# The output projection of six blocks: seven half-size products in float32 replaced by three full-size passes in float32r

## The chip, the core and the metric

The kernel runs on one NeuronCore of a Trainium2 chip. The core has a matrix engine (TensorE, "PE" in the profile; its weight loads are listed apart as "PEld"), a vector engine (VectorE, "DVE"), a scalar engine (ScalarE, "ACT"), a general engine (GpSimd, "POOL") and a queue from which most transfers are issued (SyncE, "SP"). Every engine takes its instructions in the order of the program; engines wait for each other through semaphores. SBUF is the on-chip memory, PSUM the banks that PE writes its sums to, DRAM the memory off the core. The metric is the device time of one execution, in microseconds (us).

## The reference

The input x has 4 sequences of 1024 rows of 512 float32 numbers. The part that matters here, with D = 512 and rows as tokens:

```python
h   = layernorm(x)
q, v, g = h @ Wq.T, h @ Wv.T, silu(h @ Wg.T)
ret = scan over the tokens of a sequence: state = lam * state + v
y   = (layernorm(q * ret) * gamma + lnb) * g
o   = y @ Wo.T                                  # the output projection
x1  = x + layernorm(o)
out = x1 + layernorm(ffn(layernorm(x1)))        # gate and up 512 -> 1536, down 1536 -> 512
```

The weights of the feed-forward part are rounded to 8-bit floats first; all else is float32, and the results have to agree with float32.

## The kernel before

**Blocks and turns.** The 4096 rows are 8 blocks of 512. The main loop (`for t in range(NB)`) makes 8 turns of 12 steps `i`. Turn t does the feed-forward part `f` of block t. Between its matmuls stands the attention part `b` (class `Retention`) of block t+1, the end `l` of the feed-forward part of block t-1 (scaling, normalising, adding, storing), and the preparation `n` of block t+2 (loading x, normalising, turning). The order of all instructions on each engine is the order in which this loop writes them. A step is: the matmuls `gate(i)` (8), a gap for a piece of `b`, `up(i)` (8), DVE's `fuse(i)` with a cast on ACT and later the remainder `rest(i)` on DVE, the "mid" gap, `down(i-2)` (8), and in some steps an "end" gap. `gate` and `up` take turns in two PSUM banks; ACT's silu frees the one, DVE's fuse the other.

**The attention part of blocks 2 to 7** (`fast`) uses two ways for v, q and g. Blocks 2 and 3 use a Winograd scheme in plain float32: seven products of half-size matrices per projection, taken from the list `order`, each 8 matmuls over 128x256, with DVE adds (`mids`) between them that read a PSUM bank before the next product adds to it. Blocks 4 to 7 (`by_parts`) use three float32r passes: each operand is cut by a mask into an upper part of 12 bits and a low rest. Pass "top" multiplies the upper parts, "low" the low parts (scaled), ACT scales the bank by 1 + 2^-12, and "diff" adds the product of two differences. A float32r matmul is one instruction over 128x512. For x the parts are made by `low_of` (mask and subtraction on DVE) and `diff_of` (DVE); for the weights by the class `Splitter` in turns 1 to 3, which stores them in DRAM.

**The output of blocks 2 to 7** is made in turns 1 to 6 by the Winograd scheme (`("o", j)`, function `product`): `y_sums` makes four sums of pieces of y (two on DVE, two on POOL), seven products stand in the gaps of steps 7 to 9, and `add_o` moves each bank into the SBUF tile `mids` (two copies on ACT, five adds on DVE). `o_moments`, `x1_of` then take mean and variance, normalise on ACT and add to x on POOL. The weights' sums are made once, in step 0 of turn 1 (`output_sums`: four DVE subtractions), and stored in DRAM.

**The ring.** The streamed weights of v, q, g and o come through a ring of four slots in SBUF (`fetch_weights`, `next_unit`). A load is issued on SP when the use of an earlier unit is written; SP issues in order, so it also stands behind whatever SP waits for.

**What stands ahead of the output.** In steps 3 to 6 of each turn: mean of y (`halves` splits the sum into two float32r halves on ACT and DVE, `mean` multiplies them on PE), `center_y` (DVE, squares on ACT, sums on POOL), `halves` again in step 4 for the variance, `var`, a root on ACT and a reciprocal on DVE (`rstd_y`), `scale_y` in step 5, `gate_y` in step 6 (two chunks of y before `up(6)`, two after `fuse(6)`). The last piece of g is finished at the start of step 6. In steps 6 to 8 block t+2's x is normalised (ACT), turned (`send_x`: a DVE transpose, then a transfer to DRAM), fetched turned (`fetch_x`) and, for blocks 4 to 7, masked (`low_of`). In turn 1 ACT also runs 24 searches for overflow in the rounded weights (`find_over`, tiles `seen`).

**x1nT**, the feed-forward part's input (an upper part and a rest), has two buffers of the tag "x1n"; block t's is read by `gate` and `up` of turn t, block t+1's is written from step 11 of turn t.

Of the kernel before, what the change touches and what calls it, by code (L numbers as in the profile page):

```python
# [23 lines left out]
def retention_ffn_sandwich(  # L24
# [134 lines left out]
    def scratch(n):  # L159
        t = big.tile([P, 4, PW], F32, tag="x1n", name=f"scr_{n}", bufs=2)  # L160
        return [t[:, j, :] for j in range(4)]
# [175 lines left out]
    def turn_by_blocks(dst, src, tag, name):  # L337
# [24 lines left out]
    order += [("o", j) for j in (1, 2, 6, 5, 3, 7, 4)]  # L362
    banks = {
        "v": {1: 0, 6: 1, 5: 0}, "q": {1: 1, 6: 0, 5: 1},
        "g": {1: 0, 6: 0, 5: 1}, "o": {1: 0, 6: 1, 5: 0},
# [6 lines left out]
    stream = order * (PARTS - FAST)  # L372
    late_stream = [(k, c, part) for k in "vqg" for c in range(NC) for part in ("top", "low", "diff")]
    late_stream += [("o", j) for k, j in order if k == "o"]
    stream += late_stream * (NB - PARTS)
# [21 lines left out]
    def output_sums():  # L397

        v = woT.rearrange("(c p) f -> p c f", p=P)
        operands["o"] = {1: v[:, 0:2, 0:H], 2: v[:, 2:4, 0:H], 3: v[:, 2:4, H:D]}  # L400
        b11, b12, b21, b22 = (wo_sb[:, i : i + 2, o : o + H] for i in (0, 2) for o in (0, H))
        made["o"] = {5: b11, 7: b12, 6: b22, 4: b21}
        dve.tensor_tensor(b11, b12, b11, ALU.subtract)
        dve.tensor_tensor(b12, b22, b12, ALU.subtract)
        dve.tensor_tensor(b22, b22, b11, ALU.subtract)
        dve.tensor_tensor(b21, b21, b22, ALU.subtract)

    def copy_output_weights():

        operands["late o"] = dict(operands["o"])  # L410
        for j in (1, 2, 3):
            t = dram.tile([P, 2, H], F32, tag=f"sum_o{j}", name=f"dcopy_o{j}", bufs=1)
            sp.dma_start(t, operands["o"][j])
            operands["late o"][j] = t
# [65 lines left out]
    fetched, taken = [0], [0]  # L480
    rings = {}

    def fetch_weights():

        n = fetched[0]
        change = len(order) * (PARTS - FAST)
        if n == len(stream) or (n >= change and taken[0] < change):
            return
        if n == change:
            rings[True] = wpool.tile([P, RING, D], F32R, tag="wv_sb", name="w_ring_parts")  # L490
        ring = rings[n >= change].bitcast(F32)[:, n % RING]
        what = stream[n]
        if len(what) == 2:
            k, j = what
            unit = operands["late o" if k == "o" and n >= change else k][j]
            sp.dma_start(ring.rearrange("p (c f) -> p c f", c=2), unit)
        else:
            sp.dma_start(ring, operands[what[:2]][what[2]])
        fetched[0] += 1

    def next_unit(*what):
        n = taken[0]
        assert stream[n] == what, (stream[n], what)
        taken[0] += 1
        return rings[n >= len(order) * (PARTS - FAST)][:, n % RING]
# [10 lines left out]

    class Retention:


        def __init__(self, t, xt=None):  # L520
# [8 lines left out]
            self.made = 21 if self.by_parts else 0  # L529
            self.bank, self.top = {}, {}  # L530
# [120 lines left out]
        def end(self, k, c):  # L651
# [25 lines left out]
            else:  # L677
                act.activation(mids[:, c], bank, AF.Silu)
# [11 lines left out]
        def mid(self, c):  # L690
            return mids[:, c].rearrange("p h f -> p (h f)")

        def input_sums(self, *which, engine=pool):
# [4 lines left out]
            ts_ = [t_sums[:, k].rearrange("p c (g j) -> p c g j", j=Q) for k in range(4)]  # L698
# [10 lines left out]
        def product(self):  # L709
# [11 lines left out]
            for o in range(2):  # L721
                out_ = bank[:, o]
                if k != "o" and len(self.right[j].shape) == 4:
                    out_ = out_.rearrange("p (g j) -> p g j", j=Q)
                for c in range(2):
                    if k == "o":
                        left, right = self.left[j][:, c, ts(o, P)], w[:, c, :]
                    else:
                        left, right = w[:, c, ts(o, P)], self.right[j][:, c]
                    pe.matmul(  # L730
                        out_, left, right,
                        start=(j in (1, 6, 5) and o == 0 and c == 0), stop=True,
                        skip_group_check=True,
                    )
            fetch_weights()
            if k == "o":
                return self.add_o(j, bank)
# [24 lines left out]
        def y_sums(self, *which):  # L762
            y = self.y
            a11, a12, a21, a22 = (y[:, c : c + 2, ts(h, H)] for h in range(2) for c in (0, 2))
            if self.by_parts and 1 in which:
                self.t_sums = wpool.tile([P, 4, 2, H], F32, tag="wq_sb", name=f"t_sums_{self.t}")
            s1, s2, s3, s4 = ((self.t_sums if self.by_parts else t_sums)[:, k] for k in range(4))
            self.left = {1: a11, 2: a12, 3: s4, 4: a22, 5: s1, 6: s2, 7: s3}
            ops = {
                1: (dve, s1, a21, a22, ALU.add), 2: (dve, s2, s1, a11, ALU.subtract),  # L770
                3: (pool, s3, a11, a21, ALU.subtract), 4: (pool, s4, a12, s2, ALU.subtract),
            }
            for k in which:
                engine, dst, x, y, op = ops[k]
                engine.tensor_tensor(dst, x, y, op)

        def add_o(self, j, bank):

            by_tile = mids.rearrange("p (r s) h f -> p r s h f", r=2)
            c11, c12, c21, c22 = (by_tile[:, r, :, h, :] for r in range(2) for h in range(2))  # L780
            if j == 1:
                act.copy(c21, bank)
            elif j == 2:
                act.copy(c11, bank)
            elif j == 6:
                dve.tensor_tensor(c12, bank, c21, ALU.add)
            elif j == 5:
                dve.tensor_tensor(c22, bank, c21, ALU.add)
            elif j == 3:
                dve.tensor_tensor(c12, bank, c12, ALU.add)  # L790
            elif j == 7:
                dve.tensor_tensor(c22, bank, c22, ALU.add)
            else:
                dve.tensor_tensor(c21, bank, c21, ALU.add)
            if j in (3, 4):
                for s in (0, 1) if j == 3 else (2, 3):
                    self.po[s] = mids[:, s].rearrange("p h f -> p (h f)")

        def take(self, k, o, h, src):
# [28 lines left out]
            else:  # L828
                act.activation(mids[:, 2 * o + h], src, AF.Silu)
# [101 lines left out]
        def gate_y(self, c):  # L931
# [3 lines left out]
            elif self.fast:  # L935
                y = y.rearrange("p (h f) -> p h f", h=2)
                g = mids[:, 2 * (c // 2) : 2 * (c // 2) + 2, c % 2, :]
# [36 lines left out]
        def new_x1nT(self):  # L974


            self.x1nT = big.tile(
                [P, 2, NC, TB], F32R, tag="x1n", name=f"x1nT_{self.t}", bufs=2
            )
            self.pt = {}  # L980
# [302 lines left out]
    for t in range(NB):  # L1283
        f, n = Ffn(a), None
        fast = b is not None and b.fast
        for i in range(NI):
# [45 lines left out]
            if fast and 7 <= i < 10:  # L1332
                b.product()
            if (1, 0) < (t, i) < (3, NI):
                splitter.at(t, i, "start")
            if n and n.by_parts and i == 7:
# [3 lines left out]
                n.send_x(2)  # L1340
            if n and n.by_parts and i == 8:
                n.low_of(0)
                n.low_of(1)
            if t == PARTS - 2 and i == 9:
                for _ in range(RING - 1):
                    fetch_weights()
# [332 lines left out]
```

## Time and profile before

| | |
|---|---|
| median of 3 runs (range) | 946.67 us (945.62 to 948.26) |
| the profiled execution, its span | 943.62 us, 941.8 us |
| PE busy | 915.1 us (97%), 4022 matmuls |
| DVE, ACT, POOL busy | 677.2 (72%), 439.9 (47%), 273.3 us (29%) |
| chain that ended last | PE 58%, DVE 21%, DMA 7%, ACT 5% |
| moved to and from DRAM | 148.14 MB, mean 157 GB/s |

The profile is of one execution; its timeline gives each instruction's start from the span's beginning, its length, its engine, and what it writes and reads (`out<-in`); in brackets, how long the engine stood idle before and who released it. "x8" merges neighbours. A group in the list of costliest work gives busy time, mean length in ns, and idle time before. An engine's share of the span is an average over stages; who waits for whom in a stage is read from its timeline.

### The profile page before, as it was taken

How to read it: one execution, taken by the hardware profiler on the slowest of the kernel's cores; microseconds unless marked ns; L12 is line 12 of the kernel's file. 1: busy time of each engine (PE TensorE's matmuls, PEld its weight loads, DVE VectorE, ACT ScalarE, POOL GpSimd, SP SyncE). 2: the span in 40 equal slices, each digit the busy share in tenths (PEclk: the TensorE clock that was granted, in tenths of full speed). 3: DMA queues.
4: the chain of work that ended last, by engine and by line, in shares of the span. 5: the costliest groups of instructions: out<-in, count | busy, mean ns of one | idle time of the engine just before them, and what ended most of it. 6: DMA issues, size and time to landing. Idle time of an engine off the chain costs nothing.

```text
span 941.8 us, 11982 instructions
## 1 busy us (share of the span) xinstructions
PE 915.1 (97%) x4022; PEld 754.1 (80%) x4022; DVE 677.2 (72%) x1058; ACT 439.9 (47%) x709; POOL 273.3 (29%) x340
## 2 busy tenths in 40 slices
PE   9999999989999999999999999999999999999996
PEld 7455776678888888888788888888888888888886
DVE  5996999768787886876767856767458765647445
ACT  3556675458666216442263524535264432625323
POOL 1315131321526225240342504323052412314020
PEclk9999999999999999999999999999999999999999
DMA  9302421775638864548856465556555574514021
GB/s 308 129 23 89 134 68 67 193 243 151 189 118 224 257 212 158 199 125 261 275 193 166 125 210 157 168 153 191 174 176 169 132 224 145 157 56 129 6 90 45
DMA packets 115757, 148.14 MB, mean 157 GB/s; under 512 B 10352, under 2 KB 61040, under 8 KB 115696
## 3 DMA queue, kind: packets, MB, share of 16 engines
q1 hardware_dynamic: 114832, 146.72, 50.5%
q8 instruction: 32, 0.52, 0.2%
q10 hardware_dynamic: 864, 0.66, 0.2%
q14 instruction: 29, 0.24, 0.1%
HBM read 108.81 MB, written 42.47 MB: 161 GB/s over the span
## 4 chain that ended last, share of the span: by engine, by line
PE 58%; DVE 21%; DMA 7%; ACT 5%; POOL 3%; SPq 3%; issue 2%; DVEq 0%; ACTq 0%; POOLq 0%
PE pfu L74 11%; PE pfg L74 11%; PE pd L74 9%; PE pq L74 7%; PE pv L74 7%; PE po L74 6%; PE pg L74 5%; DVE y L74 4%; DVE scr L74 3%; SPq L74 3%; DVE st L74 3%; DMA w_ring_parts<-dlow_v 2%; DMA xnT<-mx 2%; DMA mxs<-xs 1%; POOL mv L74 1%
## 5 line engine op out<-in xcount | busy, mean ns | idle before, releaser
L74 PE MATMUL pfu<-x1nT,up_sb 128*128 128x512 f32 x768 | 189.9, 390 | 2.5 <-DVE gate L74 2.5
L74 PE MATMUL pfg<-x1nT,gate_sb 128*128 128x512 f32 x768 | 186.0, 385 | 0.6 <-DVE x1nT L74 0.5
L74 PE MATMUL pd<-down_sb,fuse 128*128 128x512 f32 x720 | 175.4, 386 | 0.0
L74 PEld LDWEIGHTS pfu<-x1nT,up_sb 128*128 128x128 f32 x768 | 144.9, 189 | 27.2 <-DVE gate L74 5.4
L74 PEld LDWEIGHTS pfg<-x1nT,gate_sb 128*128 128x128 f32 x768 | 145.1, 189 | 21.7 <-DVE x1nT L74 1.3
L74 PEld LDWEIGHTS pd<-down_sb,fuse 128*128 128x128 f32 x720 | 141.5, 197 | 14.3
L74 ACT CAST fuse<-gate 128x512 fp32r<-128x512 f32 x90 | 55.5, 616 | 160.0 <-DVE gate L74 159.9
L74 ACT ACTIVATE gate<-pfg,gs_sb 128x512 f32<-128x512 f32 x96 | 65.5, 682 | 94.7 <-PE pfg L74 94.4
L74 DVE SCALAR_TENSOR_TENSOR gate<-pfu,us_sb,gate 128x512 f32<-128x512 f32 x96 | 71.5, 745 | 42.6 <-PE pfu L74 38.9
L74 POOL TENSOR_SCALAR mv<-mv 128x1 f32<-128x1 f32 (+1 forms) x82 | 24.5, 299 | 247.1 <-DVE mv L74 243.6
L74 DVE TENSOR_TENSOR fuse<-gate,fuse 128x512 fp32r<-128x512 f32 x90 | 75.5, 839 | 5.5 <-ACT fuse L74 5.5
L74 DVE BATCH_NORM_STATS2 st<-x 128x6 f32<-128x512 f32 x64 | 43.7, 683 | 22.4 <-POOL x L74 19.8
L74 POOL TENSOR_TENSOR mv<-mv,nhalf 128x1 f32<-128x1 f32 (+1 forms) x75 | 53.3, 710 | 6.3
L74 POOL TENSOR_TENSOR ysum<-y 128x512 f32<-128x512 f32 (+1 forms) x10 | 12.0, 1196 | 144.3 <-DVE y L74 144.2
L74 DVE TENSOR_TENSOR mids<-po,mids 128x512 f32<-128x512 f32 x30 | 20.5, 683 | 38.2 <-PE po L74 38.2
L74 POOL TENSOR_TENSOR x<-x,x1n 128x512 f32<-128x512 f32 x32 | 41.8, 1309 | 15.0 <-ACT x1n L74 14.9
L74 POOL TENSOR_TENSOR d<-d,x 128x512 f32<-128x512 f32 x28 | 35.7, 1296 | 16.5 <-ACT d L74 14.6
L74 POOL TENSOR_TENSOR sqsum<-sqsum,sq 128x512 f32<-128x512 f32 x24 | 34.8, 1448 | 14.6 <-ACT sq L74 12.8
L74 POOL TENSOR_TENSOR ysum<-ysum,y 128x512 f32<-128x512 f32 (+1 forms) x20 | 22.1, 1103 | 47.1 <-DVE y L74 46.7
L74 DVE RECIPROCAL rstd<-rstd 128x512 f32<-128x512 f32 x8 | 26.8, 3352 | 10.7 <-ACT rstd L74 10.7
L74 DVE TENSOR_TENSOR y<-pq,y 128x512 f32<-128x512 f32 x18 | 12.4, 690 | 28.0 <-PE pq L74 28.0
L74 ACT ACTIVATE scr<-scr,neg_low 128x1024 f32<-128x1024 f32 x18 | 20.6, 1144 | 25.5 <-DVE scr L74 25.3
(202 smaller groups left out, 1629.6 us busy)
## 6 DMA issues: line engine op xcount, KB each, us to landing
kept<-x SPq DMA_DIRECT2D x32, 256.0 KB, 2.8
x<-kept SPq DMA_DIRECT2D x32, 256.0 KB, 4.5
x<-in_x SPq DMA_DIRECT2D x28, 256.0 KB, 4.3
out<-d SPq DMA_DIRECT2D x27, 256.0 KB, 2.0
mx<-xs SPq DMA_DIRECT2D x18, 256.0 KB, 2.1
xnT<-mx SPq DMA_DIRECT2D x32, 128.0 KB, 4.7
w_ring_parts<-dtop_v SPq DMA_DIRECT2D x16, 256.0 KB, 3.7
w_ring_parts<-dlow_v SPq DMA_DIRECT2D x16, 256.0 KB, 3.0
```

The lines of the kernel that those rows point to most:

```text
L74: return lambda *args, **kwargs: tc.keep_in_program_order(op(*args, **kwargs))
```

## The change

The output of blocks 2 to 7 is made by three float32r passes, as v, q and g of blocks 4 to 7 are.

- `split_output` (turn 1, steps 0 and 1, two chunks each) makes the three parts of Wo: a mask, a subtraction and a combination on DVE, a copy on ACT, a scaling on POOL. The upper and low parts stay in SBUF, in the first buffer of x1nT; the differences go to DRAM. `output_sums`, the storing of its sums and `copy_output_weights` are gone.
- x1nT of blocks 1 to 7 has one buffer; `new_x1nT` moves from step 8 to step 11.
- `gate_y` of all four chunks stands at the start of step 6. `split_y` (four masks and subtractions on DVE, four copies on ACT) follows `fuse(6)`; `rest_of_y` (four DVE operations) follows `fuse(7)`, ahead of the last `send_x` of step 7.
- `o_gap` puts 48 matmuls into eight gaps of steps 7 to 9. The passes of token tile s go to PSUM bank s mod 2; after pass "low" ACT scales the bank. `o_moments` and `x1_of` read PSUM. They stand in step 8 (start) for tile 0, step 8 (mid) for tile 1; the moments of tile 3 move to the mid of step 9.
- The ring carries four differences per block for o in place of seven units; all four slots are held until the last tile's pass in step 9. When the ring's kind of unit changes (float32 to float32r or back), loading starts once all units of the old kind have been used.
- `mids`, and the sums of x, are taken per block from the tags of wg and wq.
- `halves` for the variance stands before the mid gap of step 4, no longer after it. The end block's `add` of tiles 2 and 3 moves from step 4 to step 5, except in turn 2.

The core of the diff:

```diff
-        t = big.tile([P, 4, PW], F32, tag="x1n", name=f"scr_{n}", bufs=2)
+        t = big.tile([P, 4, PW], F32, tag=f"x1n{n}", name=f"scr_{n}")
...
-    order += [("o", j) for j in (1, 2, 6, 5, 3, 7, 4)]
...
-    late_stream += [("o", j) for k, j in order if k == "o"]
+    last_rests = [("o", c, "diff") for c in range(NC)]
+    by_three = [(k, c, part) for k in "vqg" for c in range(NC) for part in ("top", "low", "diff")]
+    stream = (order + last_rests) * (PARTS - FAST) + (by_three + last_rests) * (NB - PARTS)
...
+    def split_output(c):
+        if c == 0:
+            room = big.tile([P, 2, NC, D], F32R, tag="x1n0", name="wo_parts")
+            wo_parts["top"], wo_parts["low"] = room[:, 0], room[:, 1]
+        w, top, low = wo_sb[:, c], wo_parts["top"][:, c], wo_parts["low"][:, c]
+        cut = work.tile([P, D], F32, tag="tok", name=f"wo_top_{c}", bufs=4)
+        dve.tensor_scalar(cut.bitcast(I32), w.bitcast(I32), TOP_MASK, None, ALU.bitwise_and)
+        dve.tensor_tensor(in_turn(low), as_read(w), as_read(cut), ALU.subtract)
+        act.copy(in_turn(top), as_read(cut))
+        dve.scalar_tensor_tensor(w, top.bitcast(F32), -LOW, low.bitcast(F32), ALU.mult, ALU.add)
+        pool.tensor_scalar(low, low.bitcast(F32), 1.0 / LOW, 1.0, ALU.mult, ALU.mult)
+        t = dram.tile([P, D], F32, tag=f"diff_o{c}", name=f"ddiff_o{c}", bufs=1)
+        sp.dma_start(t, w)
+        operands["o", c] = {"diff": t}
...
+    def fetch_weights(count=1):
+        done[0] += count
+        while fetched[0] < min(done[0] + RING, len(stream)):
+            n = fetched[0]
+            what = stream[n]
+            if n == 0 or len(what) != len(stream[n - 1]):
+                if 0 < n > done[0]:
+                    return
...
+    o_gaps = [
+        [("top", 0), ("top", 1)], [("low", 0), ("low", 1)], [("diff", 0)], [("diff", 1)],
+        [("top", 2), ("low", 2)], [("top", 3), ("low", 3)], [("diff", 2)], [("diff", 3)],
+    ]
...
+        def split_y(self, *chunks):
...
+            for c in chunks:
+                y = self.y[:, c, :]
+                top = work.tile([P, TB], F32, tag="ret", name=f"y_top_{self.t}_{c}")
+                dve.tensor_scalar(top.bitcast(I32), y.bitcast(I32), TOP_MASK, None, ALU.bitwise_and)
+                dve.tensor_tensor(self.y_low[:, c, :], y, top, ALU.subtract)
+                act.copy(self.y_top[:, c, :], top)
+        def rest_of_y(self):
+            self.y_diff = big.tile([P, NC, TB], F32R, tag="y", name=f"y_diff_{self.t}")
+            for c in range(NC):
+                dve.scalar_tensor_tensor(
+                    self.y_diff[:, c, :], self.y_low[:, c, :].bitcast(F32), -1.0 / LOW,
+                    self.y_top[:, c, :].bitcast(F32), ALU.mult, ALU.add,
+                )
...
+        def o_pass(self, part, s):
+            if part == "top":
+                self.po[s] = ps_tile(f"po_{self.t}_{s}", f"pa{s % 2}")
+            left = {"top": self.y_top, "low": self.y_low, "diff": self.y_diff}[part]
+            for c in range(NC):
+                if part != "diff":
+                    w = wo_parts[part][:, c]
+                else:
+                    if s == 0:
+                        self.o_rests[c] = next_unit("o", c, "diff")
+                    w = self.o_rests[c]
+                pe.matmul(
+                    as_read(self.po[s]), left[:, c, ts(s, P)], in_turn(w),
+                    start=part == "top" and c == 0, stop=True, skip_group_check=True,
+                )
+                if part == "diff" and s == NS - 1:
+                    fetch_weights()
+            if part == "low":
+                act.activation(self.po[s], self.po[s], AF.Copy, scale=1.0 + LOW)
...
             if fast and 7 <= i < 10:
-                b.product()
+                b.o_gap(3 * i - 21)
...
+            if fast and i == 8:
+                b.o_moments(0)
+                b.x1_of(0)
             if n and n.by_parts and i == 8:
                 n.low_of(0)
                 n.low_of(1)
...
             if fast and i == 6:
-                b.gate_y(2)
-                b.gate_y(3)
+                for c in range(NC):
+                    b.gate_y(c)
...
-            if fast and i == 7:
-                b.y_sums(3, 4)
...
+            if fast and i == 11:
+                b.new_x1nT()
             f.fuse(i)
...
             if fast and i == 9:
                 b.o_moments(2)
-                b.o_moments(3)
...
+            if fast and i == 4:
+                b.halves()
             if fast and i < 6:
                 b.gap(3 * i + 1, 2 if i == 1 else 1)
...
-            if fast and i == 4:
-                b.halves()
-                l.add(2)
-                l.add(3)
...
+            if fast and i == (4 if t == 2 else 5):
+                l.add(2)
+                l.add(3)
             if fast and i == 6:
-                b.gate_y(0)
-                b.gate_y(1)
-                b.y_sums(1, 2)
+                b.split_y(*range(NC))
+            if fast and i == 7:
+                b.rest_of_y()
...
             if n and n.by_parts and i == 7:
                 n.send_x(3)
-            if fast and i in (7, 8):
-                b.product()
+            if fast and 7 <= i < 10:
+                b.o_gap(3 * i - 20)
+            if fast and i == 9:
+                b.o_moments(3)
             if n and n.by_parts and i == 7:
                 n.fetch_x(0)
...
+            if fast and i == 8:
+                b.o_moments(1)
+                b.x1_of(1)
             if n and n.by_parts and i == 8:
                 n.low_of(2)
                 n.low_of(3)
...
             if fast and i in (7, 8):
-                b.product()
+                b.o_gap(3 * i - 19)
...
+            if t == 1 and i < 2:
+                split_output(2 * i)
+                split_output(2 * i + 1)
             if t == 1 and i == 0:
-                output_sums()
                 splitter = Splitter()
-            if t == 1 and i == 1:
-                keep_sums("o")
-            if t == 1 and i == 10:
-                copy_output_weights()
```

## The prediction

> **What bounds the kernel now.** First the page: busy time by engine, and the granted clock.
>
> ```profile
> PE 915.1 (97%) x4022; PEld 754.1 (80%) x4022; DVE 677.2 (72%) x1058; ACT 439.9 (47%) x709; POOL 273.3 (29%) x340
> PEclk9999999999999999999999999999999999999999
> ```
>
> TensorE is the bound, at full clock: a matmul taken away is time, and so is each new wait of PE. Where DVE stands relative to PE decides the rest, and the share of 72% cannot say that. So, second, the timeline of turn 5 (steps 6 to 8), which repeats to 0.1 us in turns 3 and 4.
>
> ```profile
> 718.68 1.41 DVE L74 SCALAR_TENSOR_TENSOR y<-y,lnb_sb,mids 128x512 f32<-128x512 f32 x2
> 721.05 1.70 PEld L74 LDWEIGHTS po<-w_ring_parts,y 128*128 128x128 f32 x8
> 726.17 0.69 DVE L74 STREAM_TRANSPOSE xs<-xn 128x512 f32<-128x512 f32 x1
> 728.51 1.80 SPq L74 DMA_DIRECT2D xnT<-mx  x4
> 734.16 0.42 DVE L74 TENSOR_SCALAR top<-xnT 128x512 int32<-128x512 int32 x1
> ```
>
> y is finished at 720.1, 0.95 us before PE loads its first output product. DVE has been busy without a gap since the reciprocal at 705.6, so it cannot be earlier. In turns 1 and 2 y is late already (PE waits 0.8 us for it); in turn 6 it ends at 829.4 for 830.34. The xnT load starts after the last transpose, and DVE masks it 5.7 us later.
>
> Third, the groups, for prices.
>
> ```profile
> L74 ACT CAST fuse<-gate 128x512 fp32r<-128x512 f32 x90 | 55.5, 616 | 160.0 <-DVE gate L74 159.9
> ...
> L74 DVE TENSOR_TENSOR low<-xnT,top 128x512 fp32r<-128x512 f32 x16 | 11.1, 692 | 0.5
> ...
> L74 DVE SCALAR_TENSOR_TENSOR diff<-low,top 128x512 fp32r<-128x512 f32 x16 | 10.2, 678 | 0.0
> ...
> L74 DVE TENSOR_SCALAR top<-xnT 128x512 int32<-128x512 int32 x16 | 6.7, 421 | 2.1 <-DMA xnT<-mx 2.0
> ```
>
> Fourth, the timeline of step 4 in turn 2, for the variance.
>
> ```profile
> 365.52 0.63 ACT L74 CAST half<-sqsum 128x512 fp32r<-128x512 f32 x1
> 365.80 0.69 DVE L74 TENSOR_TENSOR mids<-pg,mids 128x512 f32<-128x512 f32 x1 [1.16 <-PE pg L74]
> ...
> 366.41 1.65 DVE L74 TENSOR_TENSOR half<-sqsum,half 128x512 fp32r<-128x512 f32 x1
> ...
> 367.12 1.70 PEld L74 LDWEIGHTS pg<-t_sums,w_ring 128*128 128x128 f32 x8
> ```
>
> The add reads the bank that the product at 367.12 adds to: it must be read first. Fifth, the timeline of turn 5 around step 10, SyncE alone.
>
> ```profile
> 750.75 3.74 SPq L74 DMA_DIRECT2D mxs<-xs  x8
> 754.66 2.77 SPq L74 DMA_DIRECT2D x1n<-mxs  x2
> 757.47 0.91 SPq L74 DMA_DIRECT2D kept<-x  x2
> 758.42 0.47 SPq L74 DMA_DIRECT2D w_ring_parts<-dlow_v  x1
> ```
>
> Whatever stands behind the x1n loads is issued some 7 us after the transposes.
>
> **The change part by part.** *Work.* Eight weight loads take 1.70 us (7 intervals and a load of 0.19), so a matmul takes 0.216 us, both 128x256 in float32 and 128x512 in float32r. Seven products of 8 matmuls become 3 passes of 16: 56 become 48, -1.73 us in each of six turns, **-10.4**. The waits of PE within today's products go too (spacing of weight loads over 0.216): 0.8 in turn 1, 0.8 and 2.1 in turn 2, 0.5, 0.5 and 0.3 in turns 3 to 5, **-5.1**. The Winograd adds (five of 0.69, y's sums 0.69 and 1.65 on DVE; 1.71 and 1.28 on POOL; two copies on ACT) go, but stand behind the point where PE waits next.
>
> *A: split_y.* It stands on DVE behind the four gates and step 6's fuse, the same work that ends at 720.1 today. A chunk (mask 0.42, subtraction 0.69) takes 1.06 from start to start, as low_of's chunks do (734.16, 735.22); the fourth chunk's top is there after 3 x 1.06 + 0.42, and ACT's copy (0.62, the cast's row, and 0.05 to get there) ends at 720.1 + 4.27 = 724.37. PE is ready at 721.05, takes chunks as they come, and ends five matmuls after the last: 725.45, not 722.78. Wait 2.67 in turns 3 to 5. Turn 6: the fuse waits for PE until 827.3, the fourth copy ends at 832.3, wait 1.33. Turns 1 and 2: the gate of chunk 0 now comes first and waits for the last silu (269.94 and 385.02), and y's end plus fuse is 273.55 and 388.6; the waits are 5.69 and 5.64. Sum **+20.7**. Bounds: 17.0 (copies beside the masks cost nothing) and 24.6 (the first matmul waits for all four chunks). I take the middle: PE's rows show waits within a product, chunk by chunk (turn 1's 0.46 and 0.34).
>
> *B: rest_of_y* comes behind fuse 7 on DVE, four of 0.63; the first difference pass waits 0.3 to 0.5 for the last: **+2.3** over five turns, from 0 up.
>
> *C: the banks.* Today the sums sit in SBUF; now tiles 2 and 3 wait until x1_of has read banks 0 and 1. Tile 0 is read in time (some 736.0 for 736.3, on turn 5's scale). Tile 1's moments stand on DVE behind fuse 8, and that behind low_of for block t+2. low_of needs xnT, xnT's load the last transpose, and this now stands behind rest_of_y: 732.2, not 726.9. From the load's issue to the mask took 5.2 us in turn 2 where DVE did wait for it (396.69 to 401.86). Issued 0.5 after the transpose, xnT is there at 737.9; two low_of (2 x 1.06) and fuse 8 (0.75) end at 740.8, moments 0.87, POOL 0.9, ACT 0.3 + 0.8: bank 1 is free at 743.75, PE (725.45 and 64 matmuls, 13.8, and B) is there at 739.75. Wait 4.0 in turns 2 to 5, 0.45 in turn 6. In turn 1 ACT has its overflow searches (1.75 each, two in step 7 and one at the start of step 8) ahead of x1_of 0: waits of 3.35 and 0.4. Sum **+20.2**. Bounds: 3.6 (xnT and ACT in time: about 0.5 a turn) and 25.4 (the load also waits for the last transpose's landing, 1.3 more). I take the chain, since turn 2 already shows DVE waiting there.
>
> *D: halves sooner.* In turns 1 and 2 the half (1.65 beside POOL) goes ahead of the add, which ends at 368.55 instead of 366.49; the product that overwrites its bank starts 1.45 late. In turns 3 to 6 ACT's half goes ahead of its scaling of g 1; the difference pass, the silu, the table load (1.28) and the root follow 0.5 late, and with them DVE's reciprocal and A; PE's wait for the half (0.97) goes, but PE waits in A all the same. **+4.4**; bounds -3.9 (that wait is saved in four turns) and +4.4. I take the upper end: both queues are strict in these rows. The adds of l's tiles 2 and 3 move past nothing that POOL has to do, and x's loads pass two stores on SyncE: nothing, since POOL idles there.
>
> *E: split_output* (turn 1, steps 0 and 1). DVE gets 4 x (0.42 + 0.69 + 0.69) for 4 x 0.69, and each third operation waits for an ACT copy that stands behind three searches:
>
> ```profile
> 224.23 1.58 ACT L74 ACTIVATE seen<-up_sb,neg_max 128x1536 fp8e4<-128x1536 f32 x1
> ...
> 228.05 1.70 PEld L74 LDWEIGHTS pq<-t_sums,w_ring 128*128 128x128 f32 x8
> ```
>
> ACT is about 1 us later than here after the first two copies, so copy 2 ends at 227.7 and DVE's splits at 230.3. Behind them stand the rest (0.6), four scalings (2.48) and the add (0.69) that frees the bank of the product at 228.05: 234.1. **+6.1**; bounds 2 (copies not held up) and 7.3.
>
> *F: the ring.* Its four slots hold the output's differences until step 9's last pass; the next block's first weights are then issued behind the x1n loads. From up 9's end: fuse and moments 1.7, transposes 1.3, mxs and x1n 6.2, landing 3.7: 13.0, with PE at the first pass of v after 11.2. +1.7 in turns 1 to 5 = 8.5. Today's waits there (1.6 and 0.2, 0.7, 1.5, 0.9 at v's second low part) go, since that part is then asked for early: -4.8. **+3.7**; bounds -4.8 and +13.
>
> *The single x1nT buffer* costs nothing: its first write of a turn already follows up 11, its last reader (309.8 after 306.6 in turn 1).
>
> Sum: -10.4 - 5.1 + 20.7 + 2.3 + 20.2 + 4.4 + 6.1 + 3.7 = **+41.9**. The profiled execution took 943.62 (span 941.8), 3.05 under the median of the runs shown, which spread over 2.6: 985.5 on its scale, 988.6 on the median's. I say 987.
>
> A rule to weigh: the longest wait of PE in this profile is 2.62 us (188.44), and the clock of that stretch (184 to 190) is granted at 1.00. The waits of C and E are longer than any row here, and by rows they cost their length alone. [...]
>
> **The rivals.** *Only the first wait is real* (0.20): xnT and ACT come in time (C 3.6), E is 2, D and F nothing: -15.5 + 20.7 + 2.3 + 3.6 + 2 = +13.1, 960. For it: DVE is idle 28% and catches up in each wait of PE. Against: its work stands in one order, without a gap where it matters.
> *Faster* (0.06): split_y is hidden. It would have to start 3.6 us before PE is ready (4.27 less the three matmuls that do not need the fourth chunk), not 0.95; then A and B go, C is small with them, and -15.5 - 4.8 + 3.6 = -16.7: 930. Against: no gap of DVE after 705.6.
> *The upper ends of A, C, E and F together* (0.12): 3.9 + 5.2 + 1.2 + 9.3 more, 1007.
>
> **How the numbers follow.** The main case has 0.60, no change 0.02. A measurement of this kernel can tell about 0.3%. Faster 0.06, same 0.02, slower 0.92. The range leaves out the faster case, a third of the first rival and half of the last: 955 to 1001. The likeliest one's own range is 972 to 1001.
>
> **What would show it.** PE: 48 matmuls a turn on po, none of 128x256. A: PE's weight loads for po<-y_top, at step 7, wait for ACT. C: weight loads of po wait for ACT's x1n, DVE's top waits for xnT. D: at step 4 of turns 1 and 2, pg waits for DVE mids. E: a wait of some 5 us of pq for DVE at 229. F: pv's first pass waits for dtop_v. The prediction is wrong if split_y ends before PE gets there, or if xnT lands before DVE has sent all else.

## The result and the profile after

The changed kernel takes 998.04 us (median of 4, 996.55 to 1004.29) against 946.14 us of the kernel before (median of 4, 943.89 to 948.26): a ratio of 1.0561, 95% interval 1.051 to 1.0613. The forecast of 987 us was right in its sign and its range (955 to 1001); it is 11 us short. The profiled execution took 997.57 us (span 995.7), 53.95 more than the one of before.

The page of the changed kernel: busy time, the granted clock in 40 slices, and the chain of work that ended last, by engine.

```profile
PE 928.2 (93%) x3974; PEld 754.1 (76%) x3974; DVE 684.4 (69%) x1096; ACT 462.8 (46%) x749; POOL 260.2 (26%) x332
...
PEclk9999999998989999899999999999999999999999
...
PE 48%; DVE 28%; ACT 9%; DMA 6%; POOL 4%; issue 3%; SPq 1%; ACTq 0%; DVEq 0%; POOLq 0%
```

48 matmuls fewer, as counted; yet PE is busy for 13 us longer, and its share falls from 97% to 93%. DVE stands on 28% of the chain where it stood on 21%. The clock row, which was all 9 before, has three slices at 8.

The changed kernel's groups by line: what ended the idle time of PE's weight loads for the first pass, and the lengths of the weights' split.

```profile
L74 PEld LDWEIGHTS po<-wo_parts,y_top 128*128 128x128 f32 x96 | 20.2, 222 | 45.6 <-ACT x1n L74 23.7 <-ACT y_top L74 19.3
...
L74 DVE TENSOR_TENSOR wo_parts<-wo_sb,wo_top 128x512 fp32r<-128x512 f32 x4 | 5.3, 1326 | 0.1
L74 ACT CAST wo_parts<-wo_top 128x512 fp32r<-128x512 f32 x4 | 4.4, 1101 | 3.7 <-DVE wo_top L74 3.7
```

This one group holds most of the loss: 19.3 us of waiting for the copies of y's upper part (step A) and 23.7 us for `x1_of`, which frees a bank (step C).

Turn 5 of the changed kernel, PE's weight loads in step 7 (start, length, what is loaded, and in brackets the idle time before it and who ended that).

```profile
765.07 0.19 PEld L74 LDWEIGHTS po<-wo_parts,y_top 128*128 128x128 f32 x1
765.94 0.19 PEld L74 LDWEIGHTS po<-wo_parts,y_top 128*128 128x128 f32 x1 [0.69 <-ACT y_top L74]
767.00 0.19 PEld L74 LDWEIGHTS po<-wo_parts,y_top 128*128 128x128 f32 x1 [0.88 <-ACT y_top L74]
768.07 0.98 PEld L74 LDWEIGHTS po<-wo_parts,y_top 128*128 128x128 f32 x5 [0.88 <-ACT y_top L74]
769.14 3.29 PEld L74 LDWEIGHTS pfu<-x1nT,up_sb 128*128 128x128 f32 x8
```

PE takes y chunk by chunk, one each 1.06 us, and ends five matmuls after the last chunk. The eight loads after that take 3.29 us where eight take 1.70: they stand 0.427 us apart, not 0.216.

The same turn, DVE in step 8, and then PE's weight loads there.

```profile
781.55 0.97 DVE L74 TENSOR_SCALAR top<-xnT 128x512 int32<-128x512 int32 x1 [3.38 <-DMA xnT<-mx]
...
784.89 0.69 DVE L74 BATCH_NORM_STATS2 st<-po 128x6 f32<-128x512 f32 x1
```

```profile
788.55 0.73 PEld L74 LDWEIGHTS po<-wo_parts,y_top 128*128 128x128 f32 x4 [4.03 <-ACT x1n L74]
789.31 1.50 PEld L74 LDWEIGHTS po<-wo_parts,y_low 128*128 128x128 f32 x4
790.90 2.65 PEld L74 LDWEIGHTS pfg<-x1nT,gate_sb 128*128 128x128 f32 x8
```

DVE stands 3.38 us for the transfer of x; tile 1's moments follow behind the masks and `fuse`, and PE waits 4.03 us for the bank. Again loads at half pace follow. The same stretch in windows (length, then for PE, PEld, DVE, ACT and POOL the busy time and the instructions, the granted clock, the DMA share, GB/s):

```profile
786.00:789.00 3.00, 0.45 (x2) 0.42 (x3) 2.93 (x6) 1.30 (x4) 1.70 (x3) 1.00 0.00 0
789.00:793.00 4.00, 4.00 (x13) 3.21 (x12) 2.57 (x6) 0.58 (x1) 2.33 (x5) 0.57 0.17 66
```

The clock is granted at 1.00 while PE waits and at 0.57 over the 4 us after it. That is one reason why PE's busy time grew.

Turn 1, the split of the weights: DVE, then PE's weight loads.

```profile
226.35 1.50 DVE L74 TENSOR_TENSOR wo_parts<-wo_sb,wo_top 128x512 fp32r<-128x512 f32 x1
229.19 0.69 DVE L74 SCALAR_TENSOR_TENSOR wo_sb<-wo_parts 128x512 f32<-128x512 f32 x1 [1.35 <-ACT wo_parts L74]
...
232.91 2.48 DVE L74 TENSOR_TENSOR d<-pd,ds_sb 128x512 f32<-128x512 f32 x4
235.31 0.68 DVE L74 TENSOR_TENSOR mids<-pq,mids 128x512 f32<-128x512 f32 x1
```

```profile
236.04 3.06 PEld L74 LDWEIGHTS pq<-x_sums,w_ring 128*128 128x128 f32 x8 [6.01 <-DVE mids L74]
```

Turn 5 again, SyncE around step 10, and the pass of v that waits for it.

```profile
798.87 3.73 SPq L74 DMA_DIRECT2D mxs<-xs  x8
802.77 1.88 SPq L74 DMA_DIRECT2D x1n<-mxs  x2
804.69 0.43 SPq L74 DMA_DIRECT2D w_ring<-dtop_v  x1
805.17 0.43 SPq L74 DMA_DIRECT2D w_ring<-dlow_v  x1
```

```profile
810.70 0.73 PEld L74 LDWEIGHTS pv<-low,w_ring 128*128 128x128 f32 x4 [1.97 <-DMA w_ring<-dlow_v]
```

**The sum of before and after.** PE issues a weight load each 0.216 us when nothing holds it. Adding up what is over that in both traces gives each step of the prediction its measured size:

| step | predicted | measured |
|---|---|---|
| 48 matmuls fewer | -10.4 | -10.4 |
| waits in the old products | -5.1 | -5.1 |
| A, split of y (turns 1 to 6) | +20.7 | +19.6 (5.46, 5.46, 2.47, 2.47, 2.47, 1.30) |
| B, differences of y | +2.3 | 0 |
| C, banks | +20.2 | +23.5 (4.65, 4.75, 5.02, 4.02, 4.01, 1.07) |
| D, halves | +4.4 | +2.4 |
| E, split of the weights | +6.1 | +7.9 (1.89, 5.98) |
| F, ring | +8.5 - 4.8 | +8.0 - 4.8 |
| loads at half pace (0.427 us) | 0 | +13.5 |
| rest | | -1.2 |
| sum | +41.9 | +53.4 |

The sum counts up to the last weight load. The spans differ by 53.9: 0.4 us more stand behind that load.

The rest is mostly a wait at 197 us that was 2.13 and is 0.47, behind a first stretch at half pace at 189. The waits of A to F together were predicted at +57.4 and came to +56.6; that they agree this closely is partly luck, since single terms missed by up to 3.3 us in both directions. What the sum lacked is the line of the clock.

### The profile page after: what moved, and what is told of

It reads as the page before. It is cut to its first block, busy times and chain, and to the rows that moved or that the text cites. A ratio compares the mean times of both kernels' runs of the same rounds, so it can differ in the third digit from the quotient of the medians.

```text
span 995.7 us, 11937 instructions
## 1 busy us (share of the span) xinstructions
PE 928.2 (93%) x3974; PEld 754.1 (76%) x3974; DVE 684.4 (69%) x1096; ACT 462.8 (46%) x749; POOL 260.2 (26%) x332
## 4 chain that ended last, share of the span: by engine, by line
PE 48%; DVE 28%; ACT 9%; DMA 6%; POOL 4%; issue 3%; SPq 1%; ACTq 0%; DVEq 0%; POOLq 0%
PE pfu L74 10%; PE pfg L74 9%; PE pd L74 7%; PE pv L74 7%; PE pq L74 6%; DVE y L74 5%; PE po L74 4%; PE pg L74 4%; DVE st L74 3%; DVE scr L74 3%; DVE gate L74 2%; ACT x1n L74 2%; POOL mv L74 2%; DMA xnT<-mx 1%; DMA w_ring<-dlow_v 1%
## 5 line engine op out<-in xcount | busy, mean ns | idle before, releaser
L74 PE MATMUL pd<-down_sb,fuse 128*128 128x512 f32 x720 | 173.4, 383 | 0.0
L74 PEld LDWEIGHTS pfu<-x1nT,up_sb 128*128 128x128 f32 x768 | 148.6, 194 | 29.0 <-DVE gate L74 5.5
L74 POOL TENSOR_SCALAR mv<-mv 128x1 f32<-128x1 f32 (+1 forms) x82 | 26.7, 325 | 301.9 <-DVE mv L74 299.0
L74 DVE TENSOR_TENSOR fuse<-gate,fuse 128x512 fp32r<-128x512 f32 x90 | 71.1, 790 | 5.5 <-ACT fuse L74 5.5
L74 PE MATMUL po<-wo_parts,y_top 128*128 128x512 f32 x96 | 36.1, 488 | 33.2 <-ACT x1n L74 20.9
L74 PEld LDWEIGHTS po<-wo_parts,y_top 128*128 128x128 f32 x96 | 20.2, 222 | 45.6 <-ACT x1n L74 23.7
L74 POOL TENSOR_TENSOR mv<-mv,nhalf 128x1 f32<-128x1 f32 (+1 forms) x75 | 51.1, 681 | 6.2
L74 POOL TENSOR_TENSOR d<-d,x 128x512 f32<-128x512 f32 x28 | 38.6, 1400 | 16.5 <-ACT d L74 14.6
L74 DVE RECIPROCAL rstd<-rstd 128x512 f32<-128x512 f32 x8 | 26.8, 3352 | 17.5 <-ACT rstd L74 17.5
```

What stands on the lines that cost most here:

```text
L74: return lambda *args, **kwargs: tc.keep_in_program_order(op(*args, **kwargs))
```

## The experiments

All times are medians; the changed kernel's is 998.0, that of the kernel before lies at 943.9 to 946.1 in the comparisons. "Half pace" is the time over 0.216 us of loads that stand 0.427 us apart, from 185 us on: 14.8 in the changed kernel, 1.4 in the one before, where the clock was not halved there and a few loads stand so far apart by chance. The interval of the changed kernel's ratio (1.051 to 1.0613) overlaps with those of the runs 3, 5 and 6: what these three edits do is read from the waits in their traces, since their change of the time is not clear of noise.

**1. The bank freed sooner.** Tile 1's moments go ahead of the masks.

```diff
             if fast and i == 8:
-                b.o_moments(0)
-                b.x1_of(0)
+                for k in range(2):
+                    b.o_moments(k)
+                    b.x1_of(k)
...
-            if fast and i == 8:
-                b.o_moments(1)
-                b.x1_of(1)
```

> Moments and normalisation of output tile 1 stand ahead of the masks of the next x in step 8; nothing else changes. Theory (PE's waits of 4.0 to 5.0 us for bank 1 come from the moments standing behind fuse 8 and the masks, and these behind the transfer of x): bank 1 is free at about 782.4 on the changed kernel's scale of turn 5, PE gets there at 784.5, so the waits of turns 2 to 6 (4.75, 5.02, 4.02, 4.01, 1.07) and that of 2.40 in turn 1 go, -21.3, and with them the four stretches of matmuls at 0.427 us instead of 0.216 that follow them, -6.3: about 970. Rival (the wait is DVE's lateness as a whole and only moves): fuse 8 still stands behind the masks, PE waits as long at the next bank of up or of the last tiles, and the time stays above 990.

980.5 us (ratio to before 1.038, 1.0338 to 1.0422). PE's weight loads of turn 5 at the place of the wait of 4.03:

```profile
775.79 0.73 PEld L74 LDWEIGHTS po<-wo_parts,y_top 128*128 128x128 f32 x4 [0.33 <-ACT x1n L74]
```

Of C's 23.5 us, 3.3 are left, 2.25 of them bank 0's in turn 1. So C is the order on DVE, as the theory has it. But 10 of the 28 us did not come: the ring's waits (F) grew from 8.0 to 14.0, and half pace fell by only 1.0, since other waits now drew it. Turn 1 has the largest piece of F; SyncE and then PE there:

```profile
317.50 5.48 SPq L74 DMA_DIRECT2D mxs<-xs  x8
323.61 1.15 SPq L74 DMA_DIRECT2D x1n<-mxs  x2
324.80 0.94 SPq L74 DMA_DIRECT2D w_ring<-in_wvT  x2
```

```profile
329.00 2.40 PEld L74 LDWEIGHTS pv<-xnT,w_ring 128*128 128x128 f32 x8 [4.77 <-issue]
```

PE comes sooner, the queue ahead of the ring's loads does not.

**2. The upper part of y by ACT alone.** ACT's cast to float32r is the upper part (four in 2.61 us in the row below); the rest is y less that. The masks and the place behind `fuse(6)` go.

```diff
+        def top_of_y(self, c):
+            if c == 0:
+                self.y_top = wpool.tile([P, NC, TB], F32R, tag="wq_sb", name=f"y_top_{self.t}")
+            act.copy(self.y_top[:, c, :], self.y[:, c, :])
...
-                dve.tensor_scalar(top.bitcast(I32), y.bitcast(I32), TOP_MASK, None, ALU.bitwise_and)
-                dve.tensor_tensor(self.y_low[:, c, :], y, top, ALU.subtract)
-                act.copy(self.y_top[:, c, :], top)
+                dve.tensor_tensor(self.y_low[:, c, :], self.y[:, c, :], self.y_top[:, c, :], ALU.subtract)
...
                     b.gate_y(c)
+                    b.top_of_y(c)
```

> The upper part of y is ACT's rounded copy, one chunk behind each gate and ahead of fuse 6; the four masks on DVE go, the four subtractions stay behind fuse 6. Theory (the first wait is the chain fuse 6, four masks, four subtractions, four copies): in turns 3 to 5 the last copy ends 0.6 us after the last gate, 763.8 on the changed kernel's scale of turn 5, PE is there at 765.07: the wait of 2.47 goes, in turn 6 1.3; in turns 1 and 2 the last copy ends at about 408.4 for PE at 406.5 (turn 2), five matmuls remain after it, so 1.3 of 5.46 is left. -17.1, and -5.5 for the matmuls at half pace that follow: about 975. Rival (PE waits for y itself, late since the reciprocal): only the share of the masks (4 x 0.45) goes in each turn, -10, about 988.

978.9 us (1.0352, 1.0322 to 1.0381). Turn 5, ACT's copies, then PE's first pass:

```profile
750.14 2.61 ACT L74 CAST y_top<-y 128x512 fp32r<-128x512 f32 x4 [0.39 <-DVE y L74]
```

```profile
753.87 1.70 PEld L74 LDWEIGHTS po<-wo_parts,y_top 128*128 128x128 f32 x8
```

The copies end at 752.75, 1.1 us ahead of PE. Of A's 19.6 us, 2.6 are left, 1.28 in each of turns 1 and 2: -17.1, as expected. So A is the chain behind `fuse(6)`, masks and place together, and not y. Half pace fell by 4.3 (5.5 expected); C and F grew by 1 and 2, and in turn 2 step B appears, 1.17 us.

**3. The split of the weights in stages.** One chunk to a gap; what needs ACT's copy stands one gap behind it.

```diff
+    STAGES_MID = [[(0, False)], [(1, True), (2, False)], []]
+    STAGES_END = [[(0, True), (1, False)], [(2, True), (3, False)], [(3, True)]]
...
-            if t == 1 and i < 2:
-                split_output(2 * i)
-                split_output(2 * i + 1)
+            if t == 1 and i < 3:
+                for c, later in STAGES_END[i]:
+                    split_output(c, later)
```

> The split of the output weights in turn 1 is spread over the mid and end gaps of steps 0 to 2, one chunk in each, and DVE's combination of a chunk stands one gap behind ACT's copy of it. Theory (PE's waits of 1.89 and 5.98 us in steps 1 and 2 are DVE, which does two chunks in a row of 2.2 us each and more and waits 1.35 for ACT): both waits go but for some 1 us, and with the second the eight matmuls at half pace behind it (1.7): -8.5, about 989.5. Rival (DVE has no room for these 10 us in steps 0 to 2 whatever the order): half of the waits come back at other products, about 994.

991.8 us (1.0501, 1.047 to 1.0531). PE's weight loads at the place of the wait of 6.01:

```profile
231.99 2.08 PEld L74 LDWEIGHTS pq<-x_sums,w_ring 128*128 128x128 f32 x8 [3.22 <-DVE mids L74]
```

3.9 of 7.9 us are left (0.68 and 3.19), between the two forecasts and nearer to the rival's half: the last chunk still stands with the four scalings ahead of that add.

**4. The clock by itself.** PE is given matmuls whose result nobody reads, where it would stand: on the output's own bank ahead of the first pass, or on the bank that the next `gate` will fill.

```diff
+        def fill(self, bank, n):
+            for _ in range(n):
+                pe.matmul(bank, gate_sb[:, 0, :P], self.parts[0][:, 0], start=True, stop=True)
...
+                if i == 7:
+                    b.po[0] = ps_tile(f"po_{b.t}_0", "pa0")
+                    f.fill(b.po[0], [0, 24, 24, 11, 11, 11, 5][t])
                 b.o_gap(3 * i - 21)
...
+                if i == 8:
+                    f.idle_work(9, [0, 9, 18, 18, 18, 18, 4][t])
                 b.o_gap(3 * i - 19)
```

> Matmuls whose result nobody reads are put ahead of the passes that wait: 24, 24, 11, 11, 11 and 5 ahead of the first pass of turns 1 to 6 (0.216 us each, so 5.2, 2.4 and 1.1 us against waits of 5.46, 2.47 and 1.30), 9 and 9 in step 8 of turn 1, 18 in step 8 of turns 2 to 5, 4 in turn 6, 19 in step 2 of turn 1. No wait is made shorter. Theory (64 matmuls after the long waits run at 0.427 us because the clock was halved while PE stood): the granted clock stays at 1.0 from turn 1 to the end, and the 12 us of the stretches that follow these waits go (1.5 of them stand at 188, ahead of the first filler): about 986. Rival (those matmuls are slow for what they read or write, or are only drawn so): no change, 998, or more by fillers that do not fit.

986.5 us (1.0441, 1.0415 to 1.0467), 11.5 less than the changed kernel, with 199 matmuls more. Turn 1, the first pass behind its fillers and the eight loads after it, and then the clock row of the page:

```profile
285.56 1.71 PEld L74 LDWEIGHTS po<-wo_parts,y_top 128*128 128x128 f32 x8
287.30 1.70 PEld L74 LDWEIGHTS pfu<-x1nT,up_sb 128*128 128x128 f32 x8
```

```profile
PEclk9999999999999999999999999999999999999999
```

Sixteen loads stand at the undisturbed pace here; in the changed kernel the clock is halved there, from 284.24 to 291.06. Half pace is 0.8 in all, and the waits did not get shorter: the fillers and the waits that are left add up to 1.3 us more than the changed kernel's waits. So the clock is a cost of its own, as large as the missing 11 us, and it is PE's standing that brings it.

**5. The ring's loads first.** In step 9 the block with the transposes and transfers of x1n moves behind the last difference pass.

```diff
-            if fast and i == 9:
-                b.o_moments(2)
-                loads = []
-                for s in range(2):
-                    loads.append(b.move_x1n(s))
...
                 b.o_gap(3 * i - 20)
+            if fast and i == 9:
+                b.o_moments(2)
+                loads = []
+                for s in range(2):
+                    loads.append(b.move_x1n(s))
...
             if fast and i == 9:
                 b.o_moments(3)
```

> In step 9 the transposes and transfers of x1n stand behind the last difference pass of the output, so that the ring's first four loads for the next block are issued ahead of them on SyncE. Theory (PE's waits for the ring at v's first passes, 0.60, 1.86, 0.70, 2.25 and 2.55 us after the first to fifth output, are SyncE's order: ten issues of some 0.5 us and their waits stand ahead): the loads are issued some 8 us sooner and land before PE asks: -8, about 990. Rival (the loads are slow for the traffic in DRAM, or x1n, now 2 us later, makes new waits at the next turn's first gate): no gain, 998 or more.

994.3 us (1.053, 1.0491 to 1.0568). Turn 5, SyncE, then PE:

```profile
801.11 0.38 SPq L74 DMA_DIRECT2D w_ring<-dlow_v  x1
...
802.77 3.77 SPq L74 DMA_DIRECT2D mxs<-xs  x8
```

```profile
811.30 0.84 PEld L74 LDWEIGHTS pv<-xnT,w_ring 128*128 128x128 f32 x4
812.16 0.84 PEld L74 LDWEIGHTS pv<-low,w_ring 128*128 128x128 f32 x4
```

The loads are issued ahead, and of F's 8.0 us 1.1 are left: the mechanism is SyncE's order. The median fell by 3.7 only. In the profiled execution, the slowest of the four (999.4), half pace rose from 14.8 to 20.1, which takes back most of the waits saved. The granted clock of the other three (0.976 to 0.981, in the changed kernel 0.975 to 0.982) shows no such rise, so the clock does not explain the median. Why it fell by less than the waits stays open; the difference is within the spread.

**6. The halves late again.** `b.halves()` for step 4 back behind the mid gap.

```diff
-            if fast and i == 4:
-                b.halves()
             if fast and i < 6:
                 b.gap(3 * i + 1, 2 if i == 1 else 1)
+            if fast and i == 4:
+                b.halves()
```

> The variance's halves stand behind the mid gap of step 4 again, as before the change; the rest of the change stays. Theory: the waits of 0.41 us for the add in turns 1 and 2 go, and in turns 3 to 6 the waits of 0.71 and 0.93 (the difference pass of g 0 for DVE, the top pass of g 1 for the root) are replaced by the old one of 0.97 for the half and 0.18: -2.7, about 995.3. Rival (with the output's DVE work the halves come late in the old place, and y with them): 998 or more.

997.9 us (1.0565, 1.0538 to 1.0592): no gain. The waits of D went as expected (none of 0.41; 0.97 and 0.18 in place of 0.71 and 0.93), but turn 4's wait for bank 1 is longer; PE's weight loads:

```profile
673.61 1.35 PEld L74 LDWEIGHTS po<-wo_parts,y_top 128*128 128x128 f32 x4 [5.34 <-ACT x1n L74]
```

It was 4.02, and turn 2's is 5.90 for 4.75: together the 2.4 us that D gave. Half pace is 17.3. Why these two turns and not turns 3 and 5 stays open.

**7. The five edits together**, those of the runs 1, 2, 3, 5 and 6.

> The five edits of the other runs together: tile 1's moments early, ACT's rounded copy for y's upper part, the split of the weights in stages, the ring's loads ahead of x1n, the halves late. Theory (the three passes are cheaper than the seven products, and all of the loss is waits that the order of the queues makes): before less 10.4 of matmuls, less 9.9 of old waits, plus what is left: 2.6 at the first pass in turns 1 and 2, 2.3 for bank 0 in turn 1, 3.9 for the split of the weights, some 3 at the ring and at half pace: about 936. Rival (DVE and ACT as a whole are late, each wait taken away comes back at the next place): above 950.

940.1 us against 945.3: 0.9953, 0.9937 to 0.9969. Faster than before by 0.5%, and by 58 us faster than the changed kernel; the five gains one by one add up to 47 (17.5, 19.2, 6.2, 3.7, 0.2). Its page:

```profile
PE 909.5 (97%) x3974; PEld 747.1 (80%) x3974; DVE 679.4 (72%) x1072; ACT 462.0 (49%) x749; POOL 258.1 (27%) x332
...
PEclk9999999999999999999999999999999999999999
...
PE 60%; DVE 21%; ACT 8%; POOL 4%; DMA 3%; issue 3%; SPq 1%; DVEq 0%; ACTq 0%; POOLq 0%
```

The shares are back at those of before, with 48 matmuls less. So the three passes themselves are not dear; the order around them was, and the masks of y's split, which the second edit drops. It is 4 us over its forecast: besides the waits that were foreseen (3.2 for the split of the weights, 2.56 for bank 0 in turn 1, each now with 1.5 to 1.7 at half pace behind it) there are 1.2 of step B in turn 2, as in run 2, and 1.8 of short waits for ACT at the last passes of turns 2 to 5.

**8. The last chunk later.**

```diff
-    STAGES_MID = [[(0, False)], [(1, True), (2, False)], []]
-    STAGES_END = [[(0, True), (1, False)], [(2, True), (3, False)], [(3, True)]]
+    STAGES_MID = [[(2, False)], [(3, True), (0, False)], [(1, False)], [], []]
+    STAGES_END = [[(2, True), (3, False)], [(0, True)], [(1, True)], [], []]
```

> The five edits, with the split of the weights spread further: chunks 2, 3, 0 in steps 0 and 1, chunk 1 in step 2 behind its fuse, each combination one gap later. Theory (what is left of the wait in step 2 of turn 1, 3.2 us, is the last chunk, 2.3 us of DVE ahead of the add that frees the bank): 2.5 us less than with the five edits. Rival (the wait is that of the four scalings, 2.5 us, which stand there in any case): no difference.

939.6 us (0.9943, 0.9924 to 0.9961), no difference that can be told from the five. PE's weight loads in turn 1:

```profile
230.27 1.59 PEld L74 LDWEIGHTS pq<-x_sums,w_ring 128*128 128x128 f32 x8 [1.56 <-DVE mids L74]
...
238.78 1.59 PEld L74 LDWEIGHTS pq<-xnT,w_ring 128*128 128x128 f32 x8 [1.74 <-DVE mids L74]
```

3.2 became 1.5 and 1.7: the wait moved to where the chunk now stands.

**9. The searches elsewhere.**

```diff
-    look = [(2, 3), (2, 3), (2, 3), (1, 0), (0, 0), (0, 2)]
-    look += [(0, 1), (0, 2), (1, 0), (1, 0), (0, 0), (1, 0)]
+    look = [(2, 3), (2, 3), (2, 3), (1, 0), (0, 0), (1, 2)]
+    look += [(1, 1), (0, 0), (0, 0), (1, 0), (0, 1), (1, 0)]
```

> The six edits and a seventh: the three overflow searches that stood in steps 7 and 8 of turn 1 stand in steps 5, 6 and 10. Theory (the wait of 2.56 us for bank 0 in turn 1 is ACT's normalisation of tile 0 behind three searches of 1.75 us): it goes, and the seven or eight matmuls at 0.427 us behind it, 1.5 to 1.7: about 4 us less than with six edits, 935.5. Rival (steps 5 and 6 have no room on ACT: silus and the copies of y's upper part come late): the first pass of turn 1 waits 2 us longer, 938 or more.

939.4 us (10 runs; 0.9936, 0.9919 to 0.9953), no gain on the six. ACT in step 8 of turn 1, then PE:

```profile
287.86 0.20 ACT L74 ACTIVATE nb<-mv 128x1 f32<-128x1 f32 x1 [1.49 <-DVE mv L74]
```

```profile
289.93 0.73 PEld L74 LDWEIGHTS po<-wo_parts,y_top 128*128 128x128 f32 x4 [2.10 <-ACT x1n L74]
```

ACT is free now and itself waits for DVE's moments, which stand behind two transposes and a unit of the weights' splitter: two queues were late by nearly the same, and taking one away gave 0.5 us there, while the wait for bank 1 right after it is now 0.66. The half pace is gone (1.4, as in the kernel before), but the transposes of x1n in step 11 of turn 1 now wait 1.63 and 0.81 us where they waited 0.58; what holds them was not tried. The median of this version is the lowest of all, 0.6% under the kernel before, but cannot be told from that of the six.

## Why the prediction was right, and where its sizes were off

- **Work, and the old waits**: -10.4 and -5.1, both as read.
- **A**: right in mechanism and within 5% in size. The 2.67 per turn was 2.47; run 2 shows that the chain behind `fuse(6)` is all of it but 1.28 us in each of turns 1 and 2.
- **B**: nothing is seen where +2.3 was set. `rest_of_y` comes in time, chunk by chunk, as long as PE waits in A (turn 5: it ends at 776.03, and the first difference pass starts at 775.91 and needs the last chunk last); it showed only in run 2, once A was gone.
- **C**: right in mechanism (run 1), 3.3 us too small. Turns 4 and 5 hit the 4.0 of the working; turns 2 and 3 took 0.75 and 1.0 more, turn 6 0.6, and turn 1 was 2.25 and 2.40 for 3.35 and 0.4.
- **D**: 2.4 for 4.4; in turns 1 and 2 the wait is 0.41, not 1.45. In run 6 its worth was nothing; in that trace C takes back what it gives.
- **E**: 7.9 for 6.1. The wait that it named came with 5.98; the 1.89 one step earlier it did not have. The term set 0.69 for the subtraction and 0.62 for the copy, from rows that read and write in order; here both go through `in_turn` and `as_read`, and took 1.33 and 1.10 in the mean. The same two operations in order, on y, took 0.69 and 0.62 in the same trace; that the access order is the cause was not tried by itself.
- **F**: 3.2 net for 3.7, and the order on SyncE is its cause (run 5). The sign named the load of the upper part (`dtop_v`); the largest wait of turn 5 is for the low part behind it (`dlow_v`, 1.97).
- **The clock**: the step that failed. The prediction said that "by rows they cost their length alone", because the longest wait before, 2.62 us, had left the clock at 1.00. One row was too few: in the changed kernel's trace the same wait of 2.62 us, up to 188.69, is followed by a clock of 0.50 from 188.66 to 192.07. Nine stretches were halved there: two of them follow waits of some 2.5 us (188.66, 768.93), two A's waits of turns 1 and 2, 5.46 us each. The term that stood at nothing costs 13.5 us, and run 4 takes 11.5 of them back without touching a wait. With it the sum is 55.4 against 53.4 measured.
- **The rivals**: "only the first wait is real" is disproved by the 23.5 us of C; "faster" needed the split of y some 3.6 us ahead of PE; run 2 brings it there in another way, and together with the other four edits it is what came (run 7). The upper ends together (1007) did not come: E passed its bound of 7.3, but A and F stayed below the main case.

## What to carry to other kernels

Sum what PE's weight loads stand over their undisturbed spacing, step by step, in both traces; waits and half-clock loads then show as separate lines, and a change that removes one but draws the other is not misread. In the changed kernel's trace nine stretches at half clock (13.5 us of half pace) stand behind waits of PE of 2.35 us and more, in one piece or in three, though not behind every such wait; what helped here was to shorten such waits (y's in run 2: half pace 4.3 us less) or to fill them with matmuls (run 4: the time 11.5 us less). When work is replaced by cheaper work with a longer preparation, look at each in-order queue that the preparation joins (here DVE behind `fuse`, the bank's moments behind the next block's masks, the ring behind ten issues on SyncE): no single edit was enough, and with all five the kernel came out faster than before. Smaller sets of them were not run.

## What the hardware showed that was not expected

Waits of one length were dear in one place and not in another. The wait of 2.62 us at 188 stands in the trace of the kernel before and in that of the changed one: the clock behind it is 1.00 in the first and 0.50 in the second. The three pieces of 0.66, 0.85 and 0.85 us in step A are followed by a halved clock in turn 5 (768.93), and by a clock of 1.00 in turns 3 and 4.

In the clock records of the changed kernel's trace all changes up to the last matmul lie whole multiples of 3.413 us apart (188.66, 284.24, 410.53, 789.41), and the clock stays halved for 3.41 or 6.83 us. Cut at these multiples from 185 us on, with PE's standing taken from the spacing of its weight loads, the trace shows 2.12 to 3.41 us of standing in the stretch at full clock ahead of each of the nine halvings, and at most 1.92 in every other one at full clock. Of the pieces of step A, 2.12 us fell into one stretch in turn 5 (765.51 to 768.93); in turn 3 the two stretches that they fell into hold 1.58 and 0.89, in turn 4 1.30 and 1.17. That is one trace, and it does not show what sets these lengths. Between executions the clock differs too: the granted clock of the changed kernel's four is 0.975 to 0.982.
